# A conditioned attention and state-space block: bias and mask rows filled up to 128 partitions, with a new table of places

## The chip, the cores and the metric

The kernel runs on one core of a Trainium2 chip, in one launch. The metric is the device time of the core in microseconds (us). The version before took 1990.19 us (median of three runs, 1979.5 to 1998.85).

A core has five engines that run side by side, each through its own list of instructions in order: TensorE (PE in the profile, its weight loads PEld), VectorE (DVE), ScalarE (ACT), GpSimd (POOL) and SyncE (SP), which only issues DMA here. Matmuls write to PSUM, which VectorE and ScalarE read.

## What is computed

The input is x of 128 batches of 64 tokens with 256 channels, a condition of 512 values for each batch, a mask of tokens and a list of token places. There are two layers. The first is a linear attention:

```python
xn = layernorm(x, norm_scale, norm_bias)
q, k, v = xn @ Wq + bq, xn @ Wk + bk, xn @ Wv + bv
k = where(mask, -inf, k);  v = where(mask, 0, v)
q = softmax(q, over the 16 channels of a head);  k = softmax(k, over the tokens)
y = q @ (k^T v)                                        # by head, 16 heads
scale, shift = split(silu(cond) @ film_emb_W + film_emb_b)
h = layernorm(y) * (1 + scale) + shift
x = x + silu(h) @ film_out_W + film_out_b
```

The second is a gated state-space layer on the permuted tokens:

```python
shift, scale, gate = split(silu(cond) @ W_ada + b_ada)
h = (layernorm(x) * (1 + scale) + shift)[:, places]
xm, z = split(h @ W_in);  xm = silu(causal_conv4(xm))       # 512 channels
dt = softplus((xm @ W_xp)[..., :64] @ W_dt + b_dt);  B, C: 16 states each
state_t = state_(t-1) * exp(dt_t * A) + dt_t * xm_t * B_t   # 512 x 16 states
y = (state . C + xm * D) * silu(z)
out = x + gate * (y @ W_out)[:, places back]
```

## The kernel before

The batches are taken in 16 groups of eight (512 tokens). For each group `prepare` does the first layer and everything up to dt and the scan's inputs; then `scan` and `finish` run twice, for four batches each. The first group is prepared in two halves, so that scans can start earlier. `setup` loads weights and makes the modulation, the mask row and the bias rows.

In `scan`, for each of four blocks m of channels and each half x, ScalarE makes decays exp(dt * A) (`decay`), TensorE spreads dt * xm * B over the states with 64x64 matmuls into a PSUM tile `hb` (two buffers), VectorE runs the scan over it (`hs`, 1024 long), GpSimd or VectorE multiplies by C, GpSimd adds states in pairs, and TensorE sums the rest over the states into `yacc`, which `blank`, a matmul by zeros, has opened before. `dt` makes a round trip through DRAM (`dt_d`) to be laid out anew.

Bias and mask are added by TensorE, as first matmul of a sum in PSUM. A bias (bq, film_out_b, the gate's third of b_ada) is split into three bf16 rows in a tile `third`, so that no precision is lost, and multiplied by a matrix of ones with three rows (`project`, line 811, and the gate matmul gp of `setup`). The mask is one bf16 row of 0 or -1e30, `mrow`, multiplied by one row of ones in `prepare` (kp). Their neighbours in the same sum are f32 matmuls with 128 rows:

```python
pl.tensor.matmul(pp, lhsT=ones, rhs=third[bias][:, None, :].to_broadcast([3, 2, D]), start=True, stop=False)
...
pl.tensor.matmul(kp, lhsT=ones[0:1, :], rhs=mrow, start=True, stop=False)
```

The profile gives shapes of matmuls as rows*columns of the weights: 3*128 for a bias, 1*128 for the mask, 128*128 for its neighbours, 64*64 for hb, 128*64 for yacc.

The order of the work is not that of the source. `Plan.record` collects the operations as nodes; a unit (`with pl.unit()`) is one node. `Plan.order` then sorts them by a place from the table `ORDER`, one number for each node of each part, plus 100000 for each group; a node cannot come before what it needs or before a buffer of its tag is free. `emit` writes them out in that order, engine by engine, and in front of a ScalarE function of another table it puts a load of that table (line 481). As one helper issues all operations, nearly all have line 485 in the profile, and they are told apart by the names of their tiles.

Of the kernel before, what the change touches and what calls it, by code (L numbers as in the profile page):

```python
# [10 lines left out]
BF16 = mybir.dt.bfloat16  # L11
# [6 lines left out]
B, T, D, E = 128, 64, 256, 512  # L18
H, DH = 16, 16
DI, DS, DTR, DC = 512, 16, 64, 4  # L20
P = 128
NB = 8
# [29 lines left out]
        -995059, -994935, -991233, -991232, -971032, -305362, -251962, -322756, -411850,  # L52
        -986063, -990142, -990143, -319840, -998859, -981083, -301211, -813144, -997041,
        -993368, -997054, -981489, -997878, -991874, -990523, -994801, -985896, -996987,
        -976896, -968926, -971031, -990604, -951114, -969984, -895010, -466734, -997192,
        -989586, -977600, -518987, -981308, -981383, -969668, -981839, -310368, -533500,
        -603725, -543762, -668246, -536225, -991933, -452999, -398222, -997158, -999128,
        -992122, -967612, -997271, -995256, -989323, -999802, -966120, -998485, -962024,
        -982764, -947799, -855718, -999833, -976518, -980472, -650329, -609436, -705231,
        -625243, -640500, -692208, -600409, -633338, -707682, -654573, -741030, -706658,  # L60
        -655418, -970994, -779234, -930663, -808748, -971067, -934104, -875420, -796380,
        -891052, -670118, -702585, -839022, -737909, -972190, -304124, -322178, -223778,
    ],
    "first0": [
        -1000000, -991114, -529187, -994460, -994962, -999936, -999936, -998544, -999936,
        -999921, -996486, -990765, -972941, -999936, -1000000, -999905, -999936, -999936,
        -990323, -998987, -999758, -1000000, -987539, -988111, -966277, -971501, -986083,
        -957916, -994987, -986377, -974444, -950200, -952896, -986046, -972526, -957682,
        -979289, -987850, -970490, -949297, -916289, -985408, -963837, -941730, -952038,
        -930967, -907453, -907447, -928120, -884449, -861711, -935360, -959099, -906197,  # L70
        -884745, -926919, -902673, -909643, -906909, -906200, -908429, -898155, -903063,
        -813008, -868162, -912159, -899153, -999936, -997120, -990221, -999936, -1000000,
        -999792, -826771, -682771, -989347, -990592, -990016, -992211, -992211, -978429,
        -982690, -440858, -484572, -442918, -404750, -431762, -406261, -406938, -370644, 453,
        -324628, -326712, -958581, -421254, -324629, -325398, -324629, -324629, -387488,
        -324629, -844574, -838288, -326191, -325953, -324629, -324456, -325371, -319531,
        -301212, -300329, -164417, -391164, -172529, -301121, -167816, -288749, -164473,
        -231435, -167985, -147673, -163941, -164313, -139790, -307173, -146289, -147223,
        -139567, -174994, -164473, -134847, -144594, -150226, -134317, -144822, -146906,
        -134316, -147826, -134386, -140173, -134315, -152590, -134805, -134707, -133013,  # L80
        -326287, -190004, -131686, -200375, -133015, -207481, -996027, -132927, -129988,
        -147732, -133273, -106986, -885223, -132530, -108249, -140659, -133037, -101338,
        -974289, -116497, -107952, -133014, -130547, -100436, -588731, -67587, -68642,
    ],
    "first2": [
        -992121, -970995, -469874, -966966, -898627, -997610, -995358, -996945, -995684,
        -999784, -999756, -822479, -813355, -999773, -991829, -999405, -993980, -992161,
        -994087, -999400, -768764, -665327, -621700, -817491, -634769, -637890, -583888,
        -627342, -663883, -601358, -457294, -523956, -446498, -782722, -556542, -717683,
        -582039, -586409, -433401, -454285, -421287, -459329, -497809, -425655, -426154,  # L90
        -429164, -419967, -387487, -419719, -321626, -293880, -406937, -361628, -497357,
        -426940, -411887, -350269, -394780, -374539, -327849, -288748, -335565, -299633,
        -264048, -247552, -231344, -219423, -553809, -433515, -461393, -441827, -423327,
        -431823, -153333, -156188, -454096, -424751, -304161, -258938, -279273, -283415,
        -340857, -144850, -134706, -131268, -136899, -155056, -134271, -136435, -433892, -62033,
        -475762, -434892, -554380, -465884, -328157, -510237, -384539, -628574, -121233,
        -121771, -500934, -906743, -472740, -164647, -181881, -164481, -754360, -116569,
        -109561, -121834, -105660, -135210, -104940, -106021, -75578, -66547, -80773, -68153,
        -144505, -98818, -104252, -89186, -77436, -94044, -86891, -73823, -74895, -77276,
        -108505, -98473, -96861, -86338, -75448, -53191, -48981, -52833, -52458, -53800, -68746,  # L100
        -53712, -52940, -53192, -48477, -47718, -100418, -38381, -36696, -47354, -48108, -92558,
        -19487, -8631, -41476, -47273, -43456, -162871, -49575, -12810, -35339, -42049, -44442,
        -99823, -55773, -24279, -22535, -47650, -47276, -147956, -23424, -9283, -17974,
    ],
    "scan0_first": [
        -120865, -124068, -170934, -114729, -157264, -140744, -144348, -127898, -129067,
        -129989, -127899, -127899, -127899, -129721, -128420, -127899, -130112, -126212,
        -127545, -123001, -131269, -119854, -127916, -121050, -120747, -119591, -119488,
        -121118, -113493, -116255, -133828, -116899, -131781, -155644, -110142, -127352,
        -107209, -148482, -107182, -97767, -71927, -73602, -166378, -179505, -121579, -145763,  # L110
        -223859, -174668, -140039, -115465, -221507, -226578, -116919, -117786, -178418,
        -109471, -104251, -131188, -160013, -132113, -182174, -104841, -101402, -134576,
        -122952, -133100, -157663, -200867, -103701, -81454, -165240, -75780, -75177, -70895,
        -59991, -66840, -52446, -46691, -220098, -212182, -66641, -120875, -84216, -76761,
        -131705, -106189, -87210, -98308, -137660, -47822, -45811, -44148, -46513, -41466,
        -35307, -116514, -102688, -84223, -96506, -97445, -86899, -75877, -87345, -42421,
        -47885, -98442, -67950, -49102, -48133, -32010, -24280, -40836, -6778, -89597, -158454,
        -149914, -91971, -60755, -69154, -60957, -68528, -68220, -87448, -47468, -41705, -50379,
        -36554, -52487, -47823, -44566, -8825, -40147, -32038, -34806, -35854, -35060, -34559,
        -40457, -35778, -10839, -48125, -11819, -37185, -23477, -10643, -11576, -343, -13828,  # L120
        3252, -13048,
    ],
    "finish0_first": [
        119902, 130834, 106241, 130669, 155611, 110242, 163085, 199901,
    ],
    "scan1_first": [
        -456901, -387413, -14526, -516719, -513299, -12875, -509845, -408058, -26047, -29510,
        -13377, -34118, -31012, -21700, -28168, -15898, -4875, -39627, 3873, -196, -27645,
        -3096, 3893, -40692, -34987, -35317, -20276, -20046, -26901, -24954, -21857, -2642,
        -6084, -21354, 462, -20230, -32188, -12534, 7467, 4757, 20270, -48379, -603022, -621277,  # L130
        -564, 2326, -7129, 1082, -4831, 293, 1261, -47, 10767, -54002, 11634, 5265, -59324,
        1611, -101272, -21720, -13382, -22730, 4947, 3540, -1702, -24460, -32153, 11617, -5056,
        -140052, 19832, -19574, -1737, -450653, 23612, 17431, 29159, 50115, -689636, -681653,
        16124, 19670, -19267, 5128, 7806, 17400, -19876, 11507, 23613, 28261, -164586, 22490,
        4785, -152969, -571061, 25677, 29894, 22631, 25403, 22810, 22871, 36375, 33630, 30654,
        33205, -437054, 32277, 62770, 49975, -324147, 32871, 68916, 71422, 90718, -664017,
        -663325, 25400, -1923, 25998, 27044, 45042, -5988, 7799, 23275, 52173, 72647, 75439,
        30294, 31375, 76096, 28664, 38824, 33464, 39412, 44557, 42088, 38464, 21741, 80188,
# [1141 lines left out]
```

## Time and profile before

| | before |
|---|---|
| three runs, us | 1998.85, 1990.19, 1979.5 |
| profiled execution, us | 1973.82 |
| its span, us | 1971.9 |
| granted TensorE clock, mean | 0.981 |
| instructions | 32449 |
| bias and mask matmuls: kp, qp, op, gp | 34, 32, 32, 1 |
| ScalarE table loads | 177 (160 on line 481, 17 on line 485) |

The span is the time from the first to the last instruction of the profiled execution. Busy time is the sum of an engine's instructions; matmuls are pipelined and their ends are modelled, so TensorE's busy time holds some waiting between matmuls too. A list of waits names the instruction that waited, what it waited for, the total in us, how often and the longest.

### The profile page before, as it was taken

How to read it: one execution, taken by the hardware profiler on the slowest of the kernel's cores; microseconds unless marked ns; L12 is line 12 of the kernel's file. 1: busy time of each engine (PE TensorE's matmuls, PEld its weight loads, DVE VectorE, ACT ScalarE, POOL GpSimd, SP SyncE). 2: the span in 40 equal slices, each digit the busy share in tenths (PEclk: the TensorE clock that was granted, in tenths of full speed). 3: DMA queues.
4: the chain of work that ended last, by engine and by line, in shares of the span. 5: the costliest groups of instructions: out<-in, count | busy, mean ns of one | idle time of the engine just before them, and what ended most of it. 6: DMA issues, size and time to landing. Idle time of an engine off the chain costs nothing. (4 is left out here: it accounts for less than half of the span.)

```text
span 1971.9 us, 32449 instructions
## 1 busy us (share of the span) xinstructions
PE 1839.0 (93%) x11304; PEld 936.1 (47%) x11304; DVE 1775.6 (90%) x1626; ACT 1718.5 (87%) x3998; POOL 1787.2 (91%) x1519
## 2 busy tenths in 40 slices
PE   7798999999999999999999999999999999999777
PEld 5453554545455454544535454453544535454233
DVE  4589799999999999998999999899998999999796
ACT  4889899898989989898998989889798998989862
POOL 3579799999999999999999999899898999999997
PEclk9899999999999999999999999999999999999998
DMA  4311322304132130412213132220412213031220
GB/s 125 94 49 44 84 71 60 87 24 122 39 84 63 61 91 28 108 56 84 63 43 98 38 100 64 65 82 25 115 40 84 63 55 97 28 106 43 78 67 22
DMA packets 173083, 135.71 MB, mean 69 GB/s; under 512 B 30804, under 2 KB 157000, under 8 KB 172920
## 3 DMA queue, kind: packets, MB, share of 16 engines
q1 hardware_dynamic: 172920, 133.64, 23.6%
q8 instruction: 90, 1.47, 0.3%
q14 instruction: 73, 0.60, 0.1%
HBM read 98.84 MB, written 34.75 MB: 68 GB/s over the span
## 5 line engine op out<-in xcount | busy, mean ns | idle before, releaser
L485 DVE TENSOR_TENSOR_SCAN hs<-decay,hb 128x1024 f32<-128x1024 f32 x384 | 863.3, 2273 | 82.5 <-PE hb L485 37.0
L485 ACT ACTIVATE decay<-dt,nA 128x252 f32<-128x252 f32 x2048 | 858.5, 501 | 82.4 <-DMA dt<-dt_d 38.6
L485 POOL TENSOR_TENSOR hs<-hs,ct 128x1024 f32<-128x1024 f32 x384 | 899.6, 2364 | 31.7 <-DVE hs L485 28.7
L485 PE MATMUL hb<-diag,uT 64*64 64x512 f32 x4096 | 533.9, 618 | 71.4 <-DVE hs L485 66.9
L485 POOL TENSOR_TENSOR hs<-hs 128x1024 f32<-128x1024 f32 x224 | 526.1, 2362 | 13.7 <-DVE hs L485 9.9
L485 DVE TENSOR_TENSOR_SCAN hb<-decay,hb 128x1024 f32<-128x1024 f32 x128 | 291.4, 2277 | 0.0
L485 PE MATMUL yacc<-hs,fold 128*64 128x256 f32 x2304 | 287.4, 391 | 4.0 <-ACT yacc L485 2.0
L485 PEld LDWEIGHTS hb<-diag,uT 64*64 64x64 f32 x4096 | 121.7, 133 | 299.5 <-DVE hs L485 140.0
L485 PEld LDWEIGHTS yacc<-hs,fold 128*64 128x64 f32 x2304 | 166.3, 139 | 123.1 <-issue 43.9
L481 ACT ACT_TABLE_LOAD x160 | 205.3, 1283 | 3.4 <-PEq L1268 0.8
L485 DVE TENSOR_TENSOR hs<-hb,ct 128x1024 f32<-128x1024 f32 x128 | 156.1, 1220 | 4.8
L485 DVE SCALAR_TENSOR_TENSOR xz<-xp,vec,xz 128x504 f32<-128x504 f32 (+5 forms) x204 | 140.8, 700 | 13.8 <-ACT xz L485 9.2
L485 POOL TENSOR_TENSOR diag<-fold,bT 128x1024 f32<-128x1024 f32 x64 | 121.8, 1905 | 10.2 <-ACT bT L485 10.2
L485 PE MATMUL zp<-h,win 128*128 128x512 f32 (+1 forms) x272 | 123.4, 579 | 1.4 <-DVE xz L485 0.6
L485 PE MATMUL xp<-h,win 128*128 128x512 f32 (+1 forms) x272 | 119.2, 582 | 2.1 <-DVE xz L485 1.1
L485 PE MATMUL yop<-wout,xz 128*128 128x256 f32 x512 | 117.6, 383 | 0.0
L485 PEld LDWEIGHTS yop<-wout,xz 128*128 128x128 f32 x512 | 94.7, 190 | 25.0 <-ACT decay L485 11.4
L485 POOL TENSOR_TENSOR w<-dt,xz 128x512 f32<-128x512 f32 (+1 forms) x68 | 81.8, 1209 | 21.9 <-ACT dt L485 18.8
L485 ACT ACTIVATE yacc<-xz,vec 128x256 f32<-128x256 f32 x128 | 59.9, 468 | 32.6 <-PE yacc L485 32.6
L485 PEld LDWEIGHTS xp<-h,win 128*128 128x128 f32 x272 | 51.3, 194 | 69.1 <-issue 50.5
L485 PEld LDWEIGHTS zp<-h,win 128*128 128x128 f32 x272 | 48.6, 189 | 62.2 <-issue 44.0
L485 ACT ACTIVATE hT<-htp,mods 128x64 f32<-128x64 f32 x256 | 77.6, 439 | 0.2
(139 smaller groups left out, 2386.3 us busy)
## 6 DMA issues: line engine op xcount, KB each, us to landing
ct<-c_d SPq DMA_DIRECT2D x128, 256.0 KB
dt<-dt_d SPq DMA_DIRECT2D x256, 128.0 KB
dt_d<-dt SPq DMA_DIRECT2D x60, 256.0 KB
ga<-gate_d SPq DMA_DIRECT2D x64, 128.0 KB
xr<-x_d SPq DMA_DIRECT2D x32, 256.0 KB
out<-xr SPq DMA_DIRECT2D x32, 256.0 KB
xt<-in_x SPq DMA_DIRECT2D x15, 512.0 KB
x_d<-xt SPq DMA_DIRECT2D x15, 512.0 KB
```

What stands on the lines that cost most here:

```text
L481: engine.preload_act_table_set(loaded)
L485: getattr(engine, method)(*real, **kreal)
```

## The change

The ones get 128 rows, of which all but the first three are zero, and so do the three bias tiles; the mask row becomes row 0 of a tile of 128 rows, `mask_rows`, that is cleared once and keeps one buffer for all groups. The sums stay the same, as the added rows hold zeros on both sides. As the weights of ones are now shared between bias and mask, rows 1 and 2 of the mask tile, which meet ones, hold zeros too. The other part is the table `ORDER`: nearly all of its numbers, in every part, are replaced. The numbers themselves say little; they are cut here.

```diff
 ORDER = {
     "setup": [
-        -995059, -994935, -991233, -991232, -971032, -305362, -251962, -322756, -411850,
+        -996604, -970223, -971856, -967961, -952195, -301938, -211420, -273355, -151272,
...
-    ones = ctile([3, P], "ones", BF16)
-    nc.vector.memset(ones, 1.0)
+    ones = ctile([P, P], "ones", BF16)
+    nc.gpsimd.memset(ones, 0.0)
+    nc.gpsimd.memset(ones[0:3, :], 1.0)
+    mask_rows = ctile([P, TG], "mask_rows", BF16)
+    nc.gpsimd.memset(mask_rows, 0.0)
...
-    third = {n: kept([3, D], "third_" + n, BF16) for n in ("bq", "film_out_b", "b_gate")}
+    third = {n: kept([P, D], "third_" + n, BF16) for n in ("bq", "film_out_b", "b_gate")}
...
             pl.sync.dma_start(out=rest, in_=rows[:, at : at + D])
+            pl.vector.memset(dst, 0.0)
...
                 pl.tensor.matmul(
-                    pp, lhsT=ones, rhs=third[bias][:, None, :].to_broadcast([3, 2, D]),
+                    pp, lhsT=ones, rhs=third[bias][:, None, :].to_broadcast([P, 2, D]),
                     start=True, stop=False,
...
-        mrow = tile_of([1, TG], "mrow", "mrow", 1, BF16)
+        assert pl.slots.setdefault("mrow", 1) == 1
+        mrow = Ref(Buf([P, TG], lambda k, n=TG: mask_rows[:, :n], "mrow"))
         pl.sync.dma_start(
-            out=mrow, in_=mneg_d[first : first + NB, :].rearrange("(o b) t -> o (b t)", o=1)
+            out=mrow[0:1, :], in_=mneg_d[first : first + NB, :].rearrange("(o b) t -> o (b t)", o=1)
         )
...
-                pl.tensor.matmul(kp, lhsT=ones[0:1, :], rhs=mrow, start=True, stop=False)
+                pl.tensor.matmul(kp, lhsT=ones, rhs=mrow, start=True, stop=False)
```

## The prediction

> **What bounds the kernel now.** I read the busy shares first, then the engines by stretch, then who waited for whom in the middle of the run, and last the rows of TensorE around the bias and mask matmuls.
>
> ```profile
> PE 1839.0 (93%) x11304; PEld 936.1 (47%) x11304; DVE 1775.6 (90%) x1626; ACT 1718.5 (87%) x3998; POOL 1787.2 (91%) x1519
> ```
>
> Four engines are all nearly full, so no single one can be called the bound from this line. By stretch (columns: stretch, its length, busy time of PE, PEld, DVE, ACT and POOL, granted clock, DMA share, GB/s):
>
> ```profile
> 150.00:200.00 50.00, 44.83 (x256) 19.63 (x255) 47.00 (x43) 47.63 (x113) 45.30 (x49) 1.00 0.14 43
> 200.00:400.00 200.00, 191.62 (x1211) 101.87 (x1213) 179.72 (x164) 178.46 (x427) 180.32 (x172) 0.99 0.27 76
> 400.00:600.00 200.00, 193.74 (x1208) 96.15 (x1201) 188.65 (x168) 182.98 (x419) 191.07 (x146) 1.00 0.24 68
> ...
> 1850.00:1900.00 50.00, 38.23 (x262) 18.18 (x262) 40.46 (x26) 30.10 (x77) 45.95 (x22) 0.97 0.27 80
> ```
>
> From 200 to 1800 us the same group of work repeats. The eight stretches of 200 us there add up to PE 1539, POOL 1508, DVE 1494 and ACT 1458 of 1600 us: 96, 94, 93 and 91%. TensorE is the fullest, and all four together leave little. In the last 120 us there is no next group to prepare: POOL runs its multiplies almost without a break there, and TensorE has air. The waits of the vector and the GpSimd engine between 200 and 1800 us (total us, times, longest):
>
> ```profile
> DVE hs L485 <- PE hb L485: 34.1, 38, 3.2
> DVE hs L485 <- POOL hs L485: 16.9, 15, 1.2
> DVE km L485 <- PE kp L485: 10.7, 2, 9.1
> DVE hs L485 <- ACT decay L485: 10.6, 13, 0.9
> ...
> POOL hs L485 <- DVE hs L485: 34.0, 35, 3.2
> POOL diag L485 <- ACT bT L485: 10.2, 13, 0.8
> ```
>
> The scans on DVE wait most for TensorE's hb, by 0.9 us a time (34.1 / 38), and POOL then waits for the scans. So work taken from TensorE in front of an hb is time on the path; work taken from ACT is so only now and then.
>
> **Part 1: the filled-up rows.** The PE rows of one stretch (start, length, instruction), and the weight loads beside them:
>
> ```profile
> 427.85 1.95 PE L485 MATMUL hb<-diag,uT 64*64 64x512 f32 x16
> 429.73 0.39 PE L485 MATMUL kp<-mrow,ones 1*128 1x512 bf16 x1
> 430.04 1.98 PE L485 MATMUL kp<-xT,wk 128*128 128x512 f32 x4
> 431.95 1.09 PE L485 MATMUL hb<-diag,uT 64*64 64x512 f32 x8
> ...
> 428.33 0.15 PEld L485 LDWEIGHTS hb<-diag,uT 64*64 64x64 f32 x4 [0.28 <-issue]
> 428.76 0.15 PEld L485 LDWEIGHTS hb<-diag,uT 64*64 64x64 f32 x4 [0.28 <-issue]
> 429.72 0.09 PEld L485 LDWEIGHTS <-ones 1*128 1x128 bf16 x1 [0.81 <-issue]
> ```
>
> ```profile
> 496.73 1.99 PE L485 MATMUL op<-wfo,hT 128*128 128x256 f32 x8
> 498.66 0.38 PE L485 MATMUL op<-third_film_out_b,ones 3*128 3x512 bf16 x1
> 498.97 2.00 PE L485 MATMUL op<-wfo,hT 128*128 128x256 f32 x8
> ```
>
> Inside one tile shape, weight loads come every 0.43 us for four hb records, so 0.107 us a record; eight op records of 256 columns, half of a 512-column record's 0.43 (kp's loads at 430.57 and 431.00), are 8 x 0.213 = 1.71 us. Where the next instruction has another shape, its load starts only as the last matmul ends: sixteen hb take 429.73 - 427.85 = 1.88 instead of 16 x 0.107 = 1.71, and eight op take 498.66 - 496.73 = 1.93. A change of shape thus costs 0.17 to 0.22 us. After the ones matmul it costs less. From its start to its neighbour's is 0.31 us (498.97 - 498.66); its streaming is 0.214, since its median record is 384 ns for 512 columns and 277 for 256, 107 for each 256. That leaves 0.10.
>
> There are 34 kp, 32 qp, 32 op and one gp of these matmuls. With 128 rows the 99 changes behind them go: 99 x 0.10 = 9.9 us. The change in front goes only where the predecessor is a full tile. I count changes of shape in the built programs' order (64x64 for hb; 128x64 for yacc and yps; 64x128 for ap and dtp; full for the rest, pd's 96 columns among them; 32 rows for bp and now ones): 1055 before, 930 after. Of the 125, 99 are priced; the other 26, by neighbours that now stand together, give 26 x 0.19 = 5. Sum on TensorE: **-15 us**. Bounds: the wider operand is in no row. From below, its matmul costs what a 128-row bf16 one does, and the blank matmul of 256 columns has a median of 297 ns against 277: at most 99 x 0.02 = 2 us more. Its weight load may take the 0.19 us of a 128x128 f32 one instead of 0.09, which shows only behind another shape, 44 times: 4 us. I take neither, as the nearest load is the present one with the same 128 columns. So TensorE gains 9 to 16 us.
>
> One rule of the Trainium skill speaks against this gain: "TensorE: Matmul & The Clock Gate", under "The mechanism" of its Part 3, says that a weight load overlaps running matmuls only if its row group differs. A ones load of all rows would then overlap nothing, and this part would be worth nothing. The trace does not follow it: the eight full-height loads of qp are busy for 1.59 us inside 1.99 us of their own tile's matmuls.
>
> What else it adds is small. On POOL there are three memsets more (0.53 us by the blank row, 0.2, 0.1); POOL waits 3.82 us for DVE's statistics right after, which hides them; without that cover they'd cost 0.8. On DVE three memsets of 0.17 replace one; one stands ahead of the first statistics: 0.2 us of start-up. The part rows' DMAs now wait for these memsets, but film_out_b is first read at 47 us. The mask row's DMA still has one buffer and waits for the previous kp, as now.
>
> **Part 2: the places.** All instructions are the same but for one kind: ACT's table loads fall from 177 to 148.
>
> ```profile
> L481 ACT ACT_TABLE_LOAD x160 | 205.3, 1283 | 3.4 <-PEq L1268 0.8
> ```
>
> The other 17 are inserted in front of softplus. 29 x 1.283 = 37.2 us less on ACT: in a group, the Silu of the z columns stands between the exponentials in two blocks instead of three, and each block costs a load on either side. ACT has 142 us of idle time in the 1600, so most of this only becomes more idle. In the path stand the times that others are late because of ACT: DVE 10.6 (decay) + 5.8 (xz), POOL 10.2 (diag) + 7.8 (w), PE 22 (dtp 11.0, kp 5.5, qtp 3.4 and less): 56 us. A sixth of the loads goes (29 / 177), so I take a sixth of these waits: **-9 us**; the bounds are 0 and -37.
>
> The order itself has no row. Start and end stay as they are: the first hb still follows the second op unit on PE, POOL still ends on two hs sums behind a row of multiplies, and yacc, yop, rp and xr follow. In a group, yo, qp, the two qT copies and xp move by a few places; SP issues the first three dt and ct reads together instead of two and moves the mods read ahead of xt. No unit changes sides with more than a few others. What it may bring is bounded by the idle time of the fullest engine: 61 us of TensorE less what it gains. What it may cost is bounded by the worst repeated stretch: POOL idles 20 us in 200 to 400 and 9 in 400 to 600, 11 us for each 200, 88 us over the middle. I take 0, between the two.
>
> **Sum.** -15 - 9 = -24 us. The profiled execution took 1973.8 us (span 1971.9 and 1.9 around it), 16.4 below the median of the three runs, 1990.2, which lie up to 1% apart. Against its own time that gives 1950; against the median **1966**. With a kernel that spreads so, less than 1% can't be told from no change.
>
> **Rivals.** *Nothing passes through.* POOL's 1787 us do not change, it is 94% busy in the middle and 46 of 50 us at the end; if its chain with DVE sets the pace, TensorE and ACT only idle more. For it: POOL's waits for the scans equal DVE's waits for hb, 34 us, so only these can shrink. Against it: those waits end on PE. Price: a sixth of 34, -5: 1985.
>
> *Slower: scans starve for hb.* hb has two buffers, so TensorE may stay away for about two scans, 4.5 us, if both are full, and for one, 2.3 us, if not. Adding up what stands between one hb and the next at the rates above, stretches over 3.5 us go from 168 to 195, though those over 4.5 fall from 119 to 106. Place: the xp blocks (six in a row instead of four) and qp behind pd. Price: 27 more waits, of 0.9 us (the mean now) to 3.2 (the longest): 24 to 86 us. At 0.9 it eats the gain; from 1.6 us (44 / 27) the kernel is slower by 1%. At 2.0: -24 + 54 = +30: 2020.
>
> *The filled rows do not share the tile*, bf16 between f32 being a change of its own: -5 - 9 = -14: 1976. Against it: at 1958.64 the bf16 load of blank follows f32 yacc loads of its tile without a gap.
>
> **Chances.** The forecast with its neighbours beyond -1%: 0.47. Nothing passes, or the rows do not share: 0.32. Starving scans: 0.21. The range reaches down to both frees passing whole, -15 - 37 = -52: 1938; up to 2014, which leaves half of the slower case out.
>
> **What would show it.** Right: the ones rows read 128*128 and the next row starts 0.21 to 0.22 us later; TensorE's busy time falls by 10 to 16 us; 148 table loads; DVE's waits for PE hb below 30 us between 200 and 1800. Wrong: those waits at 60 us or more, POOL or DVE idle 10 us more in each 200, or the 0.31 us still there. What would make it wrong most likely is the order, the term that I set to 0.

## The result and the profile after

The changed kernel takes 1994.63 us (median of 20 runs, 1990.44 to 2006.41), the kernel before 1983.69 us in the same comparison (20 runs, 1971.46 to 1998.85). The ratio is 1.006, with a 95% interval of 1.0040 to 1.0081: slower by 0.6%, 10.9 us, where 1.2% faster, 24 us, was forecast. The profiled execution took 1992.03 us (span 1990.3) against 1973.82 (span 1971.9), so the traces have 18.4 us to explain. The granted clock was the same, 0.982 against 0.981.

Busy times, page of the kernel after:

```profile
PE 1816.4 (91%) x11304; PEld 933.3 (47%) x11304; DVE 1778.4 (89%) x1628; ACT 1685.4 (85%) x3969; POOL 1789.6 (90%) x1522
```

TensorE is busy for 22.6 us less than before, ACT for 33.1 us less. Both savings were made; the time did not follow. The groups of instructions show them (ACT's table loads, then the weight loads of ones; total busy us, mean ns):

```profile
L484 ACT ACT_TABLE_LOAD x131 | 168.1, 1283 | 2.9 <-PEq L1277 0.8
...
L488 ACT ACT_TABLE_LOAD x17 | 21.8, 1283 | 0.1
```

```profile
L488 PEld LDWEIGHTS <-ones 128*128 128x128 bf16 x99 | 9.7, 98 | 47.2 <-issue 46.0 <-PE htp L488 0.5
```

131 and 17 table loads make 148. A load of ones with 128 rows takes 98 ns. TensorE's rows around the bias and the mask, in the trace of the kernel after (start, length, instruction):

```profile
667.48 1.04 PE L488 MATMUL hb<-diag,uT 64*64 64x512 f32 x8
668.45 0.39 PE L488 MATMUL kp<-mask_rows,ones 128*128 128x512 bf16 x1
668.68 1.88 PE L488 MATMUL kp<-xT,wk 128*128 128x512 f32 x4
670.39 3.60 PE L488 MATMUL pd<-xz,wxp 128*96 128x512 f32 x8
673.83 0.38 PE L488 MATMUL qp<-third_bq,ones 128*128 128x512 bf16 x1
674.04 1.89 PE L488 MATMUL qp<-wq,xT 128*128 128x256 f32 x8
675.86 0.30 PE L488 MATMUL yacc<-blank 128*64 128x256 bf16 x2
676.09 1.95 PE L488 MATMUL hb<-diag,uT 64*64 64x512 f32 x16
```

The rows now read 128*128, and the neighbour starts 0.23 us (668.68 - 668.45) and 0.21 us (674.04 - 673.83) later, no longer 0.31. The same lines show what the new places do: between two hb, from 668.45 to 676.09, lie 7.64 us of kp, pd and qp. What DVE does meanwhile (the bracket is the idle time ahead and what ended it):

```profile
673.45 0.68 DVE L488 TENSOR_REDUCE km<-kp 128x8 f32<-128x512 f32 x1
675.97 0.69 DVE L488 TENSOR_REDUCE qm<-qp 128x32 f32<-128x512 f32 x1 [1.84 <-PE qp L488]
```

The engines by stretch, kernel after (stretch, length, busy time of PE, PEld, DVE, ACT and POOL, granted clock, DMA share, GB/s):

```profile
150.00:200.00 50.00, 45.19 (x248) 19.59 (x249) 46.78 (x43) 45.93 (x106) 43.61 (x39) 1.00 0.13 37
200.00:400.00 200.00, 184.32 (x1191) 99.81 (x1191) 176.18 (x162) 173.37 (x418) 178.31 (x169) 0.99 0.27 77
400.00:600.00 200.00, 189.76 (x1190) 95.00 (x1187) 184.96 (x166) 176.53 (x409) 188.68 (x135) 0.99 0.21 63
...
1850.00:1900.00 50.00, 41.20 (x234) 16.43 (x234) 37.77 (x23) 32.00 (x71) 45.74 (x23) 0.90 0.33 93
```

Over the eight stretches of 200 us from 200 to 1800 us all four engines are busy for less time. POOL's and DVE's idle time is the one to look at, because their work did not change: in each 200 us POOL idles 2.0 us more and DVE 2.3 us more on the mean, though one stretch of the eight (1200 to 1400 us) goes the other way for both. The loss lies in the repeated middle. In both traces the same events can be timed: the first scan of group 1 (the first group is 0) starts at 227.4 us after the change and at 230.2 before, so the start became 2.8 us shorter; up to the fourth product with z of group 2 the kernel after has lost 5.1 us, over the next twelve groups 16.7 (1400.8 us before, 1417.5 after), and behind them it wins 0.6. That sums to 18.4. Three groups with nearly full clock, before and then after:

```profile
477.00:826.10 349.10, 335.39 (x2102) 170.14 (x2094) 329.29 (x293) 320.26 (x745) 332.59 (x274) 1.00 0.25 69
```

```profile
481.10:837.40 356.30, 333.24 (x2096) 171.00 (x2095) 329.64 (x293) 313.42 (x739) 333.05 (x274) 0.99 0.23 68
```

DVE and POOL are as busy as before (329 and 333 us), but three groups take 7.2 us longer, and POOL idles 23.3 us instead of 16.5. What they wait for, kernel after, 200 to 1800 us (total us, times, longest):

```profile
POOL hs L488 <- DVE hs L488: 48.4, 69, 1.7
...
DVE hs L488 <- PE hb L488: 28.9, 37, 2.2
DVE qm L488 <- PE qp L488: 28.7, 20, 1.8
DVE xz L488 <- PE yacc L488: 19.3, 10, 5.2
...
DVE hb L488 <- ACT decay L488: 15.2, 26, 0.8
```

The wait that the prediction watched, for hb, fell (34.1 to 28.9). Longer are the waits of qm for qp (6.8 before) and of the product with z for yacc (6.4 before). The scan over hb behind decay is new in this form, but the scans that write hs waited 10.6 us for decay before and wait 1.5 now, so DVE's wait for decay grew by 6 us in all. POOL's wait for the scans rose from 34.0 to 48.4.

### The profile page after: what moved, and what is told of

Its sections match the earlier page's. It is cut to its first block, busy times and chain, and to the rows that moved or that the text cites. A ratio compares the mean times of both kernels' runs of the same rounds, so it can differ in the third digit from the quotient of the medians.

```text
span 1990.3 us, 32390 instructions
## 1 busy us (share of the span) xinstructions
PE 1816.4 (91%) x11304; PEld 933.3 (47%) x11304; DVE 1778.4 (89%) x1628; ACT 1685.4 (85%) x3969; POOL 1789.6 (90%) x1522
## 4 chain that ended last, share of the span: by engine, by line
POOL 28%; PE 26%; ACT 22%; DVE 13%; issue 6%; DMA 4%; SPq 1%; DVEq 0%; ACTq 0%; POOLq 0%
POOL hs L488 23%; ACT decay L488 12%; DVE hs L488 8%; PE hb L488 6%; PE yacc L488 4%; PE yop L488 3%; DMA dt<-dt_d 3%; PE xp L488 2%; DVE hb L488 2%; ACT kT L488 2%; PE ap L488 2%; PE zp L488 2%; POOL rt L488 1%; ACT L484 1%; DMA dt_d<-dt 1%
## 5 line engine op out<-in xcount | busy, mean ns | idle before, releaser
L488 PE MATMUL hb<-diag,uT 64*64 64x512 f32 x4096 | 540.9, 624 | 65.1 <-DVE hs L488 60.0
L488 DVE SCALAR_TENSOR_TENSOR xz<-xp,vec,xz 128x504 f32<-128x504 f32 (+5 forms) x204 | 136.1, 695 | 8.5 <-ACT xz L488 5.9
L488 PE MATMUL yop<-wout,xz 128*128 128x256 f32 x512 | 117.6, 383 | 3.8 <-ACT uT L488 3.8
L488 PE MATMUL dtp<-xd,wdt 64*128 64x512 f32 (+1 forms) x136 | 68.0, 604 | 20.8 <-ACT dt L488 18.1
L488 ACT ACTIVATE yacc<-xz,vec 128x256 f32<-128x256 f32 x128 | 59.9, 468 | 28.7 <-PE yacc L488 28.6
L488 DVE TENSOR_TENSOR xz<-yacc,xz 128x256 f32<-128x256 f32 x128 | 52.9, 414 | 32.3 <-PE yacc L488 32.3
L488 PEld LDWEIGHTS xp<-h,win 128*128 128x128 f32 x272 | 50.0, 190 | 66.6 <-issue 48.4
```

What stands on the lines that cost most here:

```text
L488: getattr(engine, method)(*real, **kreal)
```

## The experiments

All ratios are to the kernel before on the same chip in the same comparison, with 95% intervals. In the six comparisons that were made the kernel before had medians of 1975.8 to 1983.7 us, so ratios of different comparisons can be set against each other only to some 0.4%. A group's length below is the time from DVE's last product with z of one group to that of the next, over the twelve groups from group 2 on; "full" are groups in which the granted clock never fell to half. Half-clock time is what the trace's clock records show between 200 and 1800 us; the clock is the mean over all runs of a kernel where there are many, else of the profiled one.

| kernel | ratio | interval | median group, us | full groups, median (number) | half clock, us |
|---|---|---|---|---|---|
| before | 1 | | 116.4 | 115.9 (7) | 30.7 |
| after | 1.0060 | 1.0040-1.0081 | 118.1 | 117.9 (3) | 34.1 |
| e1 rows only | 0.9998 | 0.9975-1.0021 | 117.3 | 116.9 (2) | 54.6 |
| e2 places only | 1.0106 | 1.0075-1.0137 | 118.5 | 117.7 (4) | 44.4 |
| e3 rows, new start | 1.0046 | 1.0021-1.0072 | 118.4 | none | 85.3 |
| e4 rows, new middle | 1.0211 | 1.0177-1.0246 | 118.0 | 117.6 (5) | 61.4 |
| e5 rows, zero matmuls | 0.9928 | 0.9902-0.9955 | 116.1 | 116.1 (12) | 0 |
| e7 before, zero matmuls | 0.9907 | 0.9874-0.9940 | 116.1 | 116.1 (12) | 3.4 |
| e8 rows, zero matmuls elsewhere | 0.9941 | 0.9911-0.9970 | 116.2 | 116.1 (8) | 20.5 |
| e10 after, zero matmuls | 1.0076 | 1.0051-1.0102 | 118.4 | 117.6 (5) | 37.5 |
| e6 after, qp behind hb | 1.0226 | 1.0191-1.0261 | 121.1 | none | 85.3 |
| e9 after, old stretch | 1.0100 | 1.0076-1.0125 | 119.4 | 117.7 (5) | 34.1 |

### The two parts apart

e1 has the filled rows and the old table; three entries are put in for the new memsets. e2 has the new table without those entries, and the narrow rows.

```diff
 # e1: rows of the kernel after, table of the kernel before
+for at in (18, 28, 38):
+    ORDER["setup"].insert(at, -999999)
 # e2: rows of the kernel before, table of the kernel after
+for at in (38, 28, 18):
+    del ORDER["setup"][at]
```

> The filled rows with the old places (three places are added for the three memsets); 928 changes of tile shape on TensorE instead of 1055, 177 table loads as before. Theory A (the rows gain on TensorE, the new places lose more than that): faster than before by 10 to 24 us, ratio 0.988 to 0.995, TensorE's busy time some 15 us less. Theory B (the rows of 128 are themselves what costs, by their wider weight load or by a wait that they bring): 5 to 15 us slower than before, ratio 1.003 to 1.008. Theory C (the loss is at the start or the end): within 0.3% of before.

> The new places with the old operands of 3 and 1 rows (three places taken out); 148 table loads, 1084 changes of tile shape. Theory A: slower than the changed kernel by what the rows gain, so 20 to 36 us slower than before, ratio 1.010 to 1.018. Theory B: as fast as before or faster, ratio 0.985 to 1.000, through the 37 us that ACT saves. Theory C: 1.003 to 1.008 as the changed kernel.

The rows alone give nothing that can be measured: 0.9998 (1977.3 us), where 0.988 to 0.995 was expected if they gain on TensorE. The places alone cost 1.06% (1998.4 us), and with the rows added 0.6%. Whether the rows gain something with the new places is not shown by this: the two ratios come from different comparisons, their intervals meet, and the medians, 1998.4 and 1994.6 us, lie 3.8 us apart. e2's waits, 200 to 1800 us, are those of the kernel after:

```profile
POOL hs L490 <- DVE hs L490: 48.4, 71, 2.0
DVE qm L490 <- PE qp L490: 39.7, 20, 2.2
...
DVE hs L490 <- PE hb L490: 23.7, 30, 2.4
DVE xz L490 <- PE yacc L490: 15.5, 9, 5.2
DVE hb L490 <- ACT decay L490: 14.3, 26, 0.7
```

So the profile of the kernel after is shaped by its places. With the rows qm waits 11 us less, but the waits for hb and yacc are 9 us longer; the three add up to 78.9 us in e2 and 76.9 in the kernel after.

### Where in the table

e3 takes the new numbers for the start alone (setup, the first group and the preparation of the second), e4 for all the rest alone; both have the rows.

```diff
+START = "setup", "first0", "first2", "scan0_first", "finish0_first", "scan1_first", "finish1_first", "second"
+for name in START:          # here e3; e4: for every other name
+    ORDER[name] = NEW[name]
```

> The filled rows, the new places for setup, the first group and the preparation of the second, the old places from there on; 176 table loads. Theory A, with the loss in the repeated group: as the rows alone or 2 us better, ratio 0.987 to 0.995, groups 116 to 117 us apart from the third on. Theory B: 1.003 to 1.008. Theory C with a bad start: slower than the rows alone by over 5 us.

> The filled rows, the old places at the start and the new ones from the third group's preparation to the end; 149 table loads. Theory A, with the loss in the repeated group: like the changed kernel, ratio 1.003 to 1.010, groups 118 us apart. Theory B: the same. Theory C with a bad start: like before or faster, 0.99 to 1.00.

e3 came out at 1.0046 (1.0021 to 1.0072), where 0.987 to 0.995 was expected of it if only the repeated part costs; e4 at 1.0211 (1.0177 to 1.0246). In e3 the repeated groups have the old order, and yet none of the twelve ran at full clock: half-clock time is 85.3 us, with e6's the most in the table. Why a new start brings that is open. e4's ratio is not a price of the places alone: where the old start meets the new middle, the first half of group 1 ends at 334 us, where the kernel before has 301 and the kernel after 302. Behind that joint its groups take 118.0 us (full ones 117.6), as in the kernel after, so the repeated part of the table does carry the loss by group. Sums of parts cannot be made from these two.

### The clock

In e1 TensorE saves time, and the time does not move. Its trace shows where the saving went: between 200 and 1800 us TensorE is busy for 13.9 us less than before, and two of its waits take up 11.7 of them. Kernel before, then e1:

```profile
PE hb L485 <- DVE hs L485: 36.5, 45, 1.7
PE dtp L485 <- ACT dt L485: 11.0, 14, 0.8
```

```profile
PE hb L487 <- DVE hs L487: 43.1, 45, 2.2
PE dtp L487 <- ACT dt L487: 16.1, 14, 1.2
```

The first of them grew at one place, the same in each group, an hb behind the opening of an accumulator; kernel before, then e1:

```profile
504.65 0.30 PE L485 MATMUL yacc<-blank 128*64 128x256 bf16 x2
506.66 1.09 PE L485 MATMUL hb<-diag,uT 64*64 64x512 f32 x8 [1.71 <-DVE hs L485]
```

```profile
502.54 0.30 PE L487 MATMUL yacc<-blank 128*64 128x256 bf16 x2
505.04 1.09 PE L487 MATMUL hb<-diag,uT 64*64 64x512 f32 x8 [2.20 <-DVE hs L487]
```

TensorE waits here 0.49 us longer for the scan to give hb back, in each of twelve groups: 1.71 us before, 2.20 in e1. Against the start of that scan on DVE (504.33 us before, 502.70 in e1) it comes 0.48 us earlier. And a longer wait has a price of its own. e1 one group later, by windows of 3.413 us around the same place (columns as above; the granted clock is the third number from the end):

```profile
619.98:623.39 3.41, 1.21 (x11) 0.39 (x10) 3.41 (x2) 2.17 (x7) 2.58 (x15) 1.00 0.10 33
623.39:626.80 3.41, 3.41 (x15) 3.18 (x16) 2.92 (x3) 3.41 (x9) 3.33 (x4) 0.56 0.49 115
626.80:630.22 3.42, 3.42 (x28) 2.03 (x28) 2.17 (x2) 3.42 (x11) 3.42 (x3) 0.94 0.12 42
```

TensorE was busy for 1.21 of 3.41 us, and in the next window the granted clock is near a half (0.56 over a cut that misses the window's edges a little). With such windows e1's half-clock time is 54.6 us, against 30.7 before. Four kernels test whether the clock takes the gain. e5 puts zero matmuls, which add nothing to the sums, at two places of a group by e1's two waits (three ahead of the third dtp, one dtp before the wait, and eight of half the height ahead of the hb); e7 puts them into the kernel before; e8 puts as many at two places where TensorE does not wait; e10 puts e5's into the kernel after.

```diff
 # in scan, opening of yacc: 8 more blank matmuls; e8: (1, 1)
-            yacc = onto("yacc", HB * T)
+            yacc = onto("yacc", HB * T, 4 if (half, m) == (0, 2) else 0)
...
 # in prepare, ahead of dtp; e8: three such in front of pd
+            fill = 3 if m == 2 else 0
...
+                for n in range(fill):
+                    pl.tensor.matmul(
+                        vp, lhsT=blank[:DTR, :P], rhs=blank[:DTR, :TG], start=(n == 0), stop=False,
+                    )
```

> The filled rows with the old places, and at two places of each group where TensorE waited in the trace of the rows alone (the 4th dtp, for ACT's dt; the hb behind scan 2 of the first half, for DVE's hs) zero matmuls with nothing to compute: 3 of 256 columns ahead of the dtp and 8 of half the height ahead of the hb. Theory A (the freed time of TensorE becomes waits at these two places, the granted clock falls by half for 3.4 us after them, and that gives the gain back): the half-clock stretches between 200 and 1800 us fall from 14 (54.6 us) to 6 or fewer, the mean clock rises from 0.975 to 0.98 or more, and the time falls below the kernel with the rows alone, ratio to before 0.990 to 0.996. Rival B (the clock is not what took the gain; fillers only cost): clock as it was, ratio 1.000 to 1.006.

> The kernel before with the same zero matmuls at the same two places, as a control. Theory A: before has fewer half-clock stretches (6, 30.7 us), so there is less to win: ratio 0.996 to 1.002, and the kernel with rows and fillers stays ahead of it by 5 us or more. Rival B: fillers cost the same in both, ratio 1.000 to 1.006.

> The filled rows with the old places and the same amount of zero matmuls, but at two places where TensorE did not wait (in front of pd, and ahead of the hb behind scan 1 of the second half). Theory A: nothing is covered, the fillers only cost their own time, some 1.3 us a group and 20 us in all at most: half-clock stretches as with the rows alone (10 or more), ratio 1.003 to 1.010. Rival B: the same; it would speak against A if this kernel were as fast as the one with fillers at the places of the waits.

> The changed kernel with the zero matmuls that made the old places faster (3 ahead of the third dtp, 8 half-height ones on the third yacc of the first half). If the granted clock is a loss of its own in every order: the half-clock stretches between 200 and 1800 us fall from 10 to 4 or fewer, the groups stay at 117.3 to 118 us, the time falls by 5 to 12 us, ratio 0.999 to 1.004. If the new places leave their waits elsewhere than where these fillers stand, nothing is gained: ratio 1.004 to 1.010.

More work on TensorE made both old-order kernels faster: e5 0.9928 (1968.9 us), e7 0.9907 (1965.1 us). Half-clock time in the middle went to 0 and 3.4 us. Over all runs, the mean clock is 0.980 in the kernel before (94 runs of it) and 0.990 in e7; e1 has 0.975 and e5 0.985. From run to run of the kernel before, the time falls by 17.5 us for each 0.01 of clock, and e7's median is 18.3 us lower. e7 was expected at 0.996 to 1.006 and did better. So the clock was a real loss, in the kernel before as well: its groups at full clock take 115.9 us already, and e7's 116.1; what changed is that all twelve are such, where seven were. (The two profiled executions are closer, 1973.8 and 1963.6: the one of before was among its faster runs.) How large the gain is stays less sure: e7 has six runs, in the comparison in which the kernel before was slowest. Against the median of all 94 runs of the kernel before, 1978.3 us, its ratio would be 0.993.

Two parts of the theory fell. With the clock full, the rows are still worth nothing: twelve groups at full clock take 116.1 us in e5 and 116.1 in e7, and e5 is no faster than e7. The two times alone would not show it, since e5's mean clock over its runs is lower (0.985 against 0.990), which at 17.5 us for each 0.01 is some 8 us. And the place of the zero matmuls matters less than was held: e8 gained too (0.9941), where 1.003 or more was expected. Its half-clock time is 20.5 us, between e1's and e5's. In e10 nothing was gained (1.0076, half clock 37.5 us): in the new order TensorE's waits are elsewhere, as the second case of its expectation had it. Its full groups stay at 117.6 us: the places cost 1.5 to 2.0 us a group with the clock left out (117.6 against 116.1, 117.9 against 115.9).

### The stretch without an hb

e6 moves the first qp of a group behind the pair of hb that follows it. e9 moves kp ahead of the last hb before it and qp ahead of pd, which gives TensorE the old sequence there (kp, hb, qp, pd, hb pair).

```diff
 # e6
+ORDER["prepare"][52] = -114700
 # e9
+ORDER["prepare"][38] = -116400
+ORDER["prepare"][52] = -115450
```

> The changed kernel with one number of its places altered: in the repeated group the first qp unit is placed behind the pair of hb that follows it. Theory C (the new places cost because qp, now directly behind pd, keeps TensorE away from hb for 7.6 us and comes late for qm as well): DVE's waits for qp fall from 28.7 us to under 12, its waits for hb stay near 29 or fall, and the time falls by 6 to 14 us, ratio to before 0.999 to 1.003. Rival D (the loss lies in the rest of the new order, ACT's and POOL's turns among it): waits for qp fall but others (yacc, decay, hs) rise by as much, ratio 1.004 to 1.009 as without the edit.

> The changed kernel with two of its places altered, so that in the repeated group TensorE issues kp, one hb, qp, pd, hb pair, as in the kernel before, instead of hb pair, kp, pd, qp (7.6 us without an hb). Theory C (this stretch is where the new places lose): the groups without a half-clock stretch come down from 117.5-118 us to 116.0-116.5, DVE's waits for qp from 28.7 us to under 10, the time by 15 to 22 us, ratio to before 0.995 to 0.999. Rival D (the loss lies elsewhere in the new order, in the turns of ACT and yacc): waits for qp fall but the group stays at 117.3 us or more, ratio 1.002 to 1.008; what DVE saves at qm it then waits at hb, decay or yacc.

Neither gave anything back: e6 1.0226 (1.0191 to 1.0261), e9 1.0100. In e6 the dtp of the next block then waits for the late qt, 36.2 us in 13 waits, and ACT for that dtp, 56.6 us. In e9 the waits for qp are gone, but they turn up for hb and yacc (200 to 1800 us):

```profile
POOL hs L490 <- DVE hs L490: 74.4, 81, 1.7
DVE hs L490 <- PE hb L490: 62.5, 46, 3.0
...
DVE xz L490 <- PE yacc L490: 28.3, 14, 5.2
```

DVE waits 33.6 us more for hb than in the kernel after, and its full groups still take 117.7 us. So this stretch is where the new places show a wait, and not what the wait is due to. In e6 the forecast of the waits came true (qp 2.7 us, hb 14.0) and that of the time did not.

### One engine's turns

e12, e13 and e14 have the rows and the old order, but one engine takes its instructions by the new one: ACT, POOL and DVE. e15 has the new order, but TensorE goes by the old one.

```diff
+TAKEN = ('tensor', 'vector', 'gpsimd', 'sync')      # the engines with the old order; here e12
...
-            at[n] = max([ORDER[name][i] + PERIOD * g] + [at[m] for m in n.needs])
+            own = old if n.engine in TAKEN else new      # rank of n by the old and the new table
+            at[n] = max([own[n]] + [at[m] for m in n.needs])
```

> The filled rows with the old places, but ACT takes its instructions in the order of the new places (148 table loads); TensorE, DVE, POOL and the DMA queue keep the old order. Theory E (the regrouped turns of ACT, with the Silu of z in one block less, hold up decay and yacc and are what the new places cost): groups without a half-clock stretch at 117 us or more, ratio to before 1.006 to 1.014. If ACT's new turns are harmless and its saved loads help: ratio 0.994 to 1.001, and the cost lies with another engine's turns.

> The filled rows with the old places, but POOL alone takes its instructions in the new order (diag and the paired sums of hs change places, w and the sums of another scan too). If POOL's turns are what costs: groups at 117 us or more, ratio 1.006 to 1.014. If not: as the rows alone, 0.997 to 1.003.

> The filled rows with the old places, but DVE alone takes its instructions in the new order (qm behind both scans, ks, xz of a scan and the statistics by a few places). If DVE's turns are what costs: ratio 1.006 to 1.014. If not: as the rows alone, 0.997 to 1.003.

> The changed kernel, but TensorE alone takes its instructions in the old order; ACT, DVE, POOL and the DMA queue keep the new one. If TensorE's turns (kp, pd and qp in a row, the six xp blocks) are what costs: ratio 0.996 to 1.002. If the cost lies with another engine: 1.004 to 1.014, as the changed kernel or worse, since TensorE then goes out of step with the others.

The four give 1.121, 1.042, 1.048 and 1.141, four to thirteen times the 1.06% that was to be divided. So these runs don't say whose turns cost the 1.5 to 2.0 us. Nor does the edit set one engine apart cleanly, as a node still cannot come before what it needs. In e13 TensorE and DVE do run exactly as in e1, but at 304 of its 1522 places POOL has another instruction than in the kernel after; in e15 TensorE has another than in e1 at 524 of 11304, and ACT, DVE and POOL another than in the kernel after at 332, 171 and 108. What the four show is that a mix of the two tables costs far more than either, so a table's orders belong together.

### What holds a group at 116 us

If TensorE's saving is worth nothing, something else holds the group. Each of four kernels, built on e7 with its full clock, leaves out some of one engine's work in every group, at one place: by the busy times below 1.6 us on ACT, 1.7 on DVE, 1.9 on POOL and 3.0 on TensorE.

```diff
 # e11, POOL: one multiply of hs by ct cut to 128 columns
+                    few = 1 if (half, m, x, ii) == (0, 2, 0, 1) else SJ
 # e16, DVE: one scan over hb cut to 128 columns
+                    n = 128 if (half, m, x, ii) == (0, 1, 1, 1) else 2 * SJ * T
 # e17, TensorE: half of each z product
-                for k in range(KD):
+                for k in range(1):
 # e18, ACT: eight exponentials cut to 4 columns
+                    upto = 2 if (half, m, x) == (0, 2, 0) else T
```

> The kernel before with the zero matmuls, and one of POOL's multiplies by ct in each group cut from 128x1024 elements to 128x128 (scan 2 of the first half; the rest of that product is left out, so hs stays there without its factor). POOL has some 2.1 us less to do in each of 16 groups, DVE, ACT and TensorE the same. If POOL and its exchange with DVE set the pace (group 116.0 us with and without the filled rows): the group comes down to 113.9 to 115, the time by 16 to 34 us against the kernel with zero matmuls alone, ratio to before 0.974 to 0.983. If TensorE sets the pace after all: group 115.8 or more, ratio 0.988 to 0.994.

> The kernel before with the zero matmuls (group 116.0 us), and one of DVE's scans over hb in each group cut from 1024 to 128 columns (scan 1 of the first half; the rest of it is left out): DVE has some 2.0 us less in each group. If DVE, with TensorE's hb around it, holds the group: 114.0 to 114.8 us, the time 20 to 32 us below the kernel with zero matmuls, ratio 0.974 to 0.981. If no single engine holds it: group 115.3 or more, ratio 0.985 to 0.991.

> The kernel before with the zero matmuls, and the second half of each z product left out (4 matmuls of 512 columns, some 1.9 us of TensorE a group, more than the filled rows take). The prediction held that TensorE's time is on the path: then group 114.1 to 114.8, ratio 0.975 to 0.982. If TensorE only waits longer at hb, as with the filled rows: group 115.7 or more, ratio 0.988 to 0.996, with the waits of hb for hs up by about as much as was left out.

> The kernel before with the zero matmuls, and eight of ACT's 128 exponentials of decay in each group cut from 252 to 4 columns (scan 2 of the first half; the rest is left out), some 2 us of ACT a group. The prediction let a sixth of the saving on ACT through. If ACT is off the path: group 115.8 or more, ratio 0.988 to 0.994. If it holds the group together with the others: 114.3 to 115.3, ratio 0.978 to 0.986.

Three groups of e7 and then of e17, by stretch:

```profile
477.60:825.50 347.90, 337.71 (x2135) 171.20 (x2127) 329.19 (x293) 320.28 (x745) 332.84 (x274) 1.00 0.25 70
```

```profile
480.90:828.90 348.00, 328.71 (x2110) 167.07 (x2103) 329.04 (x292) 320.08 (x745) 332.51 (x274) 1.00 0.24 69
```

TensorE is busy 9.0 us less in the three groups, and they take 348.0 us instead of 347.9. (An f32 matmul of the z product has two records in the trace, of some 0.43 us each; so the four that are left out are more than the 1.9 us that the expectation names.) The others, in the same three groups: e5 348.0 (TensorE 3.4 less), e16 348.1 (DVE 5.2 less), e18 348.0 (ACT 4.9 less), e11 347.7 (POOL 5.8 less). Only POOL's saving moves the median group, from 116.1 to 115.6 us, a quarter of what was taken and between the two cases of its expectation; POOL's wait for the scans rose from 23.2 us in e7 to 42.1 in e11. The times agree: e11 1962.8 us, e16 1968.8, e17 1968.8, e18 1966.1 against e7's 1965.1 in another comparison; as ratios 0.9913 (0.9891 to 0.9936), 0.9965 (0.9943 to 0.9987), 0.9973 (0.9952 to 0.9995) and 0.9958 (0.9931 to 0.9985). The last three lie above every range that was expected; the kernel before was fastest in their comparison (1975.8 us), and the groups of 116.0 us are what to go by. These three have e7's zero matmuls and less work, so they also say that the zero matmuls gain between some 0.3% and e7's 0.9%. A third of TensorE's saving (38.6 us from 200 to 1800 us) went where half of e1's had gone, into its wait for the scans, and most of the rest into waits for ACT, of which the largest is new; e7 and then e17:

```profile
PE hb L485 <- DVE hs L485: 29.5, 42, 1.3
```

```profile
PE hb L485 <- DVE hs L485: 42.4, 44, 1.3
...
PE xp L485 <- ACT xz L485: 8.6, 13, 0.7
```

The theory of one engine that holds the group thus fell for the places that were cut; another place on the same engine was not tried. What holds the group at 116.0 stays open. POOL is the nearest, as it alone moved the group; that something else stands 0.5 us behind it is a guess from e11. One candidate that no run tried is the round trip of dt through DRAM, for which ACT's decay waits 25.7 us in e7.

The fastest version found that computes everything is e7: the kernel before with eleven zero matmuls a group, 0.9907; e5, with the rows as well, lies within its interval.

For the new order the traces hold one hint that no run followed up. The chain that the profile follows back from the last instruction lies on POOL's hs for 35.7% of the time from 480 to 826 us in the kernel after, more than on anything else, and for 12.2% in e2; in the kernel before and in e7 the chain breaks off long before these groups, so there is nothing to set beside it.

## Why the prediction was wrong, step by step

**Filled rows, TensorE -15 us: the size was about right, the passing on to the time failed.** The price of the exit was 0.10 us; the rows show 0.08 to 0.10 (0.31 down to 0.21 and 0.23). The rule that speaks against the overlap had no weight: a ones load of all rows costs no stall. TensorE's busy time fell by 13.3 us with the old places (1839.0 to 1825.7 in e1) and by 30.8 with the new ones (1847.2 in e2 to 1816.4), though busy time holds waits. What failed is the inference from the first part, "TensorE is the fullest", to "work taken from TensorE in front of an hb is time on the path". TensorE waits for DVE to give hb back as often as DVE waits for hb, and of e1's 13.9 us between 200 and 1800 us 6.6 became the first of these waits and 5.1 a longer wait for ACT's dt. With 3.0 us a group taken away in e17 the group did not move either. The prediction read one side of this loop, DVE's 34.1 us behind PE. The other side stood in the same trace of the kernel before, 200 to 1800 us:

```profile
PE hb L485 <- DVE hs L485: 36.5, 45, 1.7
...
DVE hs L485 <- PE hb L485: 34.1, 38, 3.2
```

Where each waits for the other by about as much, neither is the one that holds the pace.

**Table loads, -9 us of 37: size right, passing on not found.** 148 loads came, and ACT's busy time fell by 33. But these loads fell because the turns were regrouped, and DVE's wait for decay, of which the prediction expected a sixth to go, grew by 6 us. In e18 1.6 us a group less on ACT gave nothing in the old order. No run takes the loads alone away, so their worth in the new order is not known.

**The order, set to 0: this is the step that made the sign wrong.** With its table loads it costs about 1.06% by itself (e2), some 21 us, 1.5 to 2.0 us in each full group. The 0 was taken from between two bounds and came from no row. "No unit changes sides with more than a few others" holds for DVE, where in the traces of e1 and the kernel after an instruction of the middle changes sides with 7 others at most; on ACT qT and uT do so with up to 17 and 18, and on TensorE utp with up to 80 records. And a few places were no argument that it costs nothing: qp's move made 28.7 us of waits at qm. Which of the moves costs the 21 us stays open. The prediction named this term as its weakest, and its bounds, 61 us of gain and 88 of loss, held the value.

**The rival "scans starve for hb"** had the sign, and it had seen qp behind pd. Its mechanism was not what happened: DVE's waits for hb fell by 5 us, where they were to reach 60. On DVE qm stands ahead of the next scan in both orders, and in the new one qp comes last before that scan's hb, so the wait fell on qm. With the old stretch back (e9) the waits for hb did reach 62.5 us, in a kernel that is slower still.

**The rival "nothing passes through"** is right for the rows: no change for them was measured (e1, and e5 against e7). Its reason, POOL's chain with DVE, is half supported: POOL is the only engine whose relief moved the group at all, by a quarter of what was taken.

**What was to show it.** The 128*128 rows, the 0.21 us, the 148 loads and waits for hb under 30 us all came as for a right forecast, and TensorE's busy time fell by more than was asked (22.6 us). Of the signs of a wrong forecast none came at its size: POOL and DVE idled 2.0 and 2.3 us more in each 200, where 10 us was to be the sign. A loss of 0.6% is 1.2 us in 200, so that sign could not have shown it. Signs of a saving don't show that it reaches the end.

**Against the median.** 1994.6 lies 28.6 us above the forecast and inside the range of 1938 to 2014. The forecast started from three runs with a median of 1990.2; against the twenty of the comparison, 1983.7, the miss is 35 us, from -24 to +10.9. The difference of 0.6% is inside the 1% that had a chance of 0.32, but not for the reasons given there: the order loses some 21 us where it runs alone, and it is not that nothing passes through.

## What to carry to other kernels

Before passing an engine's saving on to the time, read both sides of its loop: if the engine that saves also waits for the one that waits for it, a saving turns into wait until some other run has shown that it does not. Price a re-sorted order by running it alone: an order is one thing for all engines, and neither a look at what moved nor one engine's turns told its price here. And where TensorE's work has holes of 2 us in a busy kernel, look at the granted clock after them: matmuls by zeros near the holes made the old order faster, by 0.3 to 0.9%, where the filled rows gave nothing that could be measured. In the new order, whose waits are elsewhere, they gave nothing.

## What was not expected of the hardware

The granted clock falls to a half in steps of 3.413 us, on a fixed grid, and it follows TensorE's idle time in the window before. In the twenty profiled executions of this study, from 200 to 1950 us, I added up TensorE's idle time in each full-clock window of that grid. Of 165 windows with 2.0 us of idle time or more, all 165 were followed by a window at half clock; of 8373 with less than 0.6 us, one was; between these it was 155 of 1268, and only from 1.8 us on more than half (37 of 61). So idle time alone does not settle the range between. In e1's window shown above all of the idle time was one wait of 2.20 us.

The Trainium skill, "TensorE: Matmul & The Clock Gate", Part 1, describes such windows, of 3413 ns, and that agrees with the records. It has the clock go back to half after an idle window of that length; here 2.0 us out of 3.41 sufficed, each of 165 times.

Over the 94 runs of the kernel before, the time follows the run's mean granted clock (correlation -0.95), and 17.5 us for each 0.01 is close to a hundredth of TensorE's 1839 us. So most of the runs' spread of some 1% goes with the clock. It looks like proof that TensorE's work is on the path, and e17 shows for one place that it is not: 3.0 us less of it in a group changed nothing. One reason may be that a window at half clock slows hb at the moment when a scan is waiting for it. That is argued from the place of the dips, and no run separates it.
